# Attention on blocks of four tokens: products of 64 and 68 columns, sums from a column of ones, exponential behind the transposing

## The chip, the cores and the metric

The kernel runs on one core of a Trainium2 chip. The metric is the device time of one execution in microseconds. Before the change the median of nine runs is 490.96 us (483.93 to 496.37).

## The reference

Four conditioned layers act in turn on x, 64 batches of 64 tokens of 256 features, all in fp32; each adds its result to x. The first is a low-rank projection modulated per batch, the second a linear map whose weights are decoded from a condition, the fourth a set of layer norms with gathered gains and an MLP over six concatenated branches. The change is in the third:

```python
kx = modulated_linear(x, s, k_aff_w, k_aff_b, k_w, k_b)
kx = kx.reshape(B, N, H, D)                      # 64 x 64 x 16 x 16
q = k = v = kx
scores = jnp.einsum('bnhd,bnjd->bnhj', q, k) / math.sqrt(D)
A = jax.nn.softmax(scores, axis=-1)
out = jnp.einsum('bnhj,bnjd->bnhd', A, v).reshape(B, N, F)
out = modulated_linear(out, s, o_aff_w, o_aff_b, o_w, o_b)
```

The attention is among the 16 heads of one token: for each of the 4096 tokens a 16x16 matrix of scores from 16 vectors of 16 elements, a softmax over its rows, and its product with the same 16 vectors.

## The kernel before

The 4096 tokens are taken in eight chunks of 512 (`CH`), and behind the keys in 16 units P of 256 (`PT`). `layers01(c)` does the first two layers of a chunk and the keys: it ends with `pt`, the keys of a unit turned so that tokens lie on the partitions, copied to `kk` by ACT. `attention(P)` follows, then `layers23(P)`, which multiplies by the output weights (`po`), norms, gathers, and does the MLP (`ph` for its six branches, `pq` for its second product).

A token's 16x16 products are too small for the tensor engine, so several tokens are put into one product with zeros around them. The keys go to DRAM (`kd`, `vd`) and come back (`fetch`) in the layouts that are needed. Before the change, eight tokens share a product. For the scores, `kb` holds the 128 contraction rows (16 elements x 8 tokens) and, for each of 32 groups, 128 columns (8 tokens x 16 heads), zero but in a token's own block; it is 16 partitions wide per token, so it takes eight transfers (L762). `kz` holds the same keys packed, 32 columns per group with zeros beside, as weights. Two products (h = 0, 1) with weights shifted by 16 columns add up in PSUM; the scores of a unit, `pS`, are 32 products with 32 weight columns and 128 streamed columns, in four column groups of 32 output partitions each (L789). The softmax follows: maximum, difference, exponential on ACT, sum, reciprocal and product on DVE, and a transposing on DVE into `at` (L796 to L803). For the values, `vb` holds 128 columns per group (8 transfers, L767), and `pv` is again 32 products of 128 columns in four column groups (L813); ACT copies it to `av` (L818), `ad` takes it to DRAM (L822), and two transfers bring it back turned as `aT` (L829). Half of what `pv` computes and `ad` carries is not used: only the blocks that belong to a token are read back. `styleq` is the output's modulation in the order of `aT`.

`kb` and `vb` are two halves of one tensor `kv`, which holds the decoder's weights `W_dec` first. There is one of each, so the fetch of unit P+1 must wait until the products of unit P have read them. `at` is one buffer, `kz` two. An fp32 product is two instructions on PE (the trace counts 64 per unit for `pS`).

PSUM has eight banks in four sets: A (2), B (3), C (2) and S (1). `pS` uses S; `pv` and `ph` share the two banks of C.

Nothing is issued as it is written. `Plan.step` takes every step with an engine, a cost, and what it reads and writes; `Plan.order` lays the steps out in time on each engine, choosing among those ready by a rank, which is the unit's base plus `LEAD` of its stage and `SHIFT` of stage and unit, and `emit` writes all the steps in that order. So each engine runs a fixed list in order, and a step that waits holds up those behind it. SP issues all the transfers but the gathers (POOL) and some first loads (ACT).

Of the kernel before, what the change touches and what calls it, by code (L numbers as in the profile page):

```python
# [18 lines left out]
NH, HD = 16, 16  # L19
# [42 lines left out]
class Plan:  # L62
# [3 lines left out]
    LANES, ISSUE, LAND, HOP, SLACK = 8, 0.54, 2.3, 0.12, 0.0  # L66
    TABLE = 1.4

    LEAD = {"down": 946.4, "fetch": 1090.6, "gather": 1168.5, "hidden": 1056.4, "keys": 938.1, "last": 1046.3,
            "load": 934.3, "load W1": 1568.6, "load W2": 1287.4, "load decoder": 1245.0, "load first": 604.2, "load ids": 902.1,  # L70
            "load keys": 911.3, "load states": 1260.1, "load up": 753.0, "mid": 546.9, "norm": 984.7, "out": 1165.7,
            "park": 927.1, "scores": 1120.2, "set W1": 1041.3, "set decoder": 215.9, "set down": 150.6, "set k": 952.6,
            "set o": 868.6, "set states": 1178.6, "turn": 1040.2, "up": 1091.5, "values": -313.8}


    SHIFT = {"down": (121.0, 0.0, -136.0, 0.0, 45.3, 0.0, 57.2, 0.0, 669.8, 0.0, 452.8, 0.0, 448.6, 0.0, 203.0, 0.0),
            "fetch": (-21.2, -95.4, 22.4, 39.5, 73.9, 129.8, -198.4, 143.2, 60.9, 236.7, -128.9, -10.1, -60.7, 22.7, -201.3, -74.5),
            "gather": (25.1, 20.6, -52.3, 44.9, 149.5, 295.4, 273.6, -73.2, 25.2, 4.2, 71.4, 347.0, 156.9, 181.1, 284.4, 233.7),
            "hidden": (-23.7, -102.8, 100.9, 97.4, -70.1, 56.9, 93.3, -244.5, -119.8, 73.4, -11.9, 193.5, 100.1, -16.4, -8.7, 2.5),
            "keys": (-138.5, 0.0, -157.5, 0.0, 320.2, 0.0, 194.1, 0.0, 169.5, 0.0, 259.2, 0.0, 207.7, 0.0, 209.6, 0.0),  # L80
            "last": (-49.6, -146.3, 100.1, 60.6, -162.7, -187.0, 32.8, 25.1, 68.0, -10.7, 96.6, -194.4, -61.8, 407.3, 397.6, 375.4),
            "load": (0.0, 0.0, 0.0, 0.0, 311.2, 0.0, 24.7, 0.0, -364.5, 0.0, 23.9, 0.0, 66.9, 0.0, 299.3, 0.0),
            "mid": (-25.3, 0.0, -351.6, 0.0, -179.2, 0.0, -1.1, 0.0, -6.1, 0.0, 131.7, 0.0, 213.3, 0.0, 249.5, 0.0),
            "norm": (-246.5, -272.7, -139.3, -283.8, -207.2, -15.7, -104.9, 40.1, -219.1, 16.5, -133.9, -101.4, -119.9, 129.5, 13.2, -265.9),
            "out": (75.9, 13.0, -112.7, -113.3, -174.2, 11.1, 82.9, 26.4, 125.1, -118.1, 220.2, -0.8, 136.4, 254.8, -8.3, 195.2),
            "park": (-302.5, 0.0, -53.5, 0.0, -775.7, 0.0, -547.9, 0.0, -550.1, 0.0, -359.8, 0.0, -152.5, 0.0, 238.3, 0.0),
            "scores": (-82.8, 70.4, 67.7, -137.7, -106.8, -38.2, 26.9, 83.3, 98.4, 82.9, 84.9, -0.6, 136.4, 144.2, 34.2, 171.0),
            "turn": (-82.0, 10.3, -20.8, -18.4, -23.5, -0.8, 77.8, 214.9, 84.7, 115.0, -41.3, 77.4, -122.1, 45.8, 69.3, 164.8),
            "up": (-344.7, 0.0, -102.1, 0.0, -238.6, 0.0, -224.7, 0.0, -115.4, 0.0, -84.9, 0.0, -54.9, 0.0, -53.0, 0.0),
            "values": (-74.2, 53.7, -70.1, -159.6, 81.8, 307.5, -59.3, -54.8, 80.6, -145.4, -166.2, -196.3, -101.8, -85.7, -218.8, 125.5)}  # L90
# [12 lines left out]
    @staticmethod  # L103
    def keys(things):
        out = []
        for t in things:
            if isinstance(t, tuple) and isinstance(t[0], Buf):
                out.append((t[0], t[1]))
            else:
                out.append((t, None))  # L110
        return out
# [147 lines left out]
def tile_kernel(ctx: ExitStack, tc: tile.TileContext, a: dict, out: bass.AP):  # L259
# [15 lines left out]
    BUFS = {"x": 3, "xr": 3, "pw": 2, "cg": 2, "mg": 2, "ei": 2, "oh": 2, "t4": 3, "kk": 2, "kc": 1, "act": 2, "E": 2,  # L275
            "aT": 2, "xt": 2, "ft": 2, "hs": 2, "y3": 2, "y1": 1, "mx": 2, "sm": 2, "tab": 2, "st": 2, "mv": 2, "rs": 2, "rsx": 2, "rsh": 2, "rsy": 2, "nmx": 2, "nmh": 2}
# [4 lines left out]
    def bank(name, tag="B"):  # L281
        return Buf(ps, tag, {"A": 2, "B": 3, "C": 2, "S": 1}[tag], [128, 512], name, turns=(tag == "A"))
# [35 lines left out]

    styleq = fixed("styleq", [128, 2, B // PB, 4, 2])
# [14 lines left out]
    kz = [fixed(f"kz{i}", [128, 32 * NG + 16]) for i in range(2)]  # L334

    kv = fixed("kv", [128, 2 * NG * 128])
    kb, vb = (kv[:, i * NG * 128 : (i + 1) * NG * 128].rearrange("p (b g j) -> p b g j", g=NG, b=8) for i in range(2))
    at_ = fixed("at", [128, 32 * NH + 16])


    def consts():
# [4 lines left out]
    step("POOL", 0.4, lambda: (nc.gpsimd.memset(neghalf, -0.5), nc.gpsimd.memset(V, 0.0), nc.gpsimd.memset(bigtab, 0.0),  # L346
                               nc.gpsimd.memset(at_[:, 32 * NH :], 0.0)),
         w=["neghalf", "V", "at0", "zeros"], rank=-107)
    step("POOL", 3.5, lambda: nc.gpsimd.memset(U, 0.0), w=["U"], rank=-108.5)
    for z in range(2):  # L350
        step("POOL", 1.0, lambda z=z: nc.gpsimd.memset(kz[z], 0.0), w=[f"kz{z}"], rank=-106)
# [419 lines left out]
    def parts(n):  # L771
        return [f"{n}.{b}" for b in range(8)]
# [274 lines left out]
```

## Time and profile before

| | |
|---|---|
| median of nine runs | 490.96 us |
| the profiled execution | 487.56 us |
| its span, first to last instruction | 485.8 us |
| mean granted clock of PE | 0.930 |
| DMA packets, bytes | 192668, 83.53 MB |
| of these under 512 B | 159819 |
| SP: `kv<-kd` (L762), 128 issues | 471 / 587 / 2190 ns (least, median, most) |
| SP: `kv<-vd` (L767), 128 issues | 302 / 420 / 1652 ns |
| SP: `vd<-kk` (L744), 64 issues | 582 / 675 / 2894 ns |
| SP: `aT<-ad` (L829), 32 issues | 364 / 505 / 1927 ns |
| ACT: exponential, 128x512 (L798) | 16, 630 ns |
| ACT: copy to `av`, 128x512 (L818) | 32, 590 ns |
| ACT: copy to `kz`, 128x512 (L756) | 16, 618 ns |
| ACT: function table load | 1283 ns each |
| DVE: sum (L799), reciprocal (L800), product (L801) | 684, 351, 690 ns |
| DVE: maximum (L796), difference (L797), transposing (L803) | 686, 691, 707 ns |

Times are those of one profiled execution. PE's row is the matmuls, PEld's the weight loads, which overlap them. A group's mean counts one instruction from start to end, while several are under way at once; its busy time is what they cover together. The waits of an engine are put down to what ended them. The chain of waits runs back from the last instruction, at each step to what released it.

### The profile page before, as it was taken

How to read it: one execution, taken by the hardware profiler on the slowest of the kernel's cores; microseconds unless marked ns; L12 is line 12 of the kernel's file. 1: busy time of each engine (PE TensorE's matmuls, PEld its weight loads, DVE VectorE, ACT ScalarE, POOL GpSimd, SP SyncE). 2: the span in 40 equal slices, each digit the busy share in tenths (PEclk: the TensorE clock that was granted, in tenths of full speed). 3: DMA queues.
4: the chain of work that ended last, by engine and by line, in shares of the span. 5: the costliest groups of instructions: out<-in, count | busy, mean ns of one | idle time of the engine just before them, and what ended most of it. 6: DMA issues, size and time to landing. Idle time of an engine off the chain costs nothing.

```text
span 485.8 us, 11060 instructions
## 1 busy us (share of the span) xinstructions
PE 417.1 (86%) x4026; PEld 317.5 (65%) x4026; DVE 311.9 (64%) x668; ACT 297.2 (61%) x875; POOL 154.2 (32%) x164
## 2 busy tenths in 40 slices
PE   3969859784996899989999998799898988999890
PEld 2956535553773678668777776687666767888770
DVE  0698994541975267587777775759683863886642
ACT  1305815639569465769379738894697964876530
POOL 5470040000436015024613540245132634255110
PEclk9989958976899599989999999999899997999997
DMA  8999676586698768658967897688677777775000
GB/s 271 309 225 276 132 191 153 137 118 152 86 189 234 205 129 201 145 155 230 197 210 115 221 190 191 147 222 131 159 181 252 137 159 208 183 217 156 23 22 22
DMA packets 192668, 83.53 MB, mean 172 GB/s; under 512 B 159819, under 2 KB 174119, under 8 KB 192615
## 3 DMA queue, kind: packets, MB, share of 16 engines
q1 hardware_dynamic: 184679, 57.81, 52.8%
q0 software_dynamic: 6656, 20.98, 15.8%
q10 hardware_dynamic: 1280, 4.05, 2.3%
q8 instruction: 32, 0.52, 0.5%
q14 instruction: 21, 0.17, 0.1%
HBM read 56.91 MB, written 25.89 MB: 170 GB/s over the span
## 4 chain that ended last, share of the span: by engine, by line
PE 51%; DVE 11%; SPq 11%; ACT 11%; DMA 10%; issue 3%; POOLq 0%; POOL 0%; ACTq 0%; DVEq 0%
PE ph L943 18%; PE pv L813 5%; PE pS L789 4%; PE po L883 4%; SPq L767 4%; SPq L762 3%; PE pq L951 3%; DMA kc<-kd 3%; PE pk L707 2%; ACT t L656 2%; PE p L637 2%; DMA aT<-ad 2%; ACT ot L886 2%; DMA kv<-vd 2%; PE pz L688 2%
## 5 line engine op out<-in xcount | busy, mean ns | idle before, releaser
L886 ACT ACTIVATE ot<-po,cols,demod_o 128x64 f32<-128x64 f32 x128 | 41.0, 427 | 14.9 <-PE po L883 14.9
L842 POOL TENSOR_TENSOR rs_x<-rs_x,neghalf 128x2 f32<-128x2 f32 x16 | 13.1, 821 | 115.3 <-DVE rs_x L841 114.8
L856 POOL DMA_INDIRECT mg<-in_ms_tab,ids x32 | 33.8, 1058 | 35.6 <-PE pfs L928 21.0
L710 ACT ACTIVATE kT<-pk,cols,demod_k 128x64 f32<-128x64 f32 x128 | 39.6, 438 | 5.6 <-PE pk L707 3.1
L883 PE MATMUL po<-aS,w_o 128*128 128x256 f32 x128 | 34.7, 419 | 7.9 <-DVE aS L877 7.9
L856 POOL DMA_INDIRECT pw<-in_pw_tab,ids x32 | 34.6, 1082 | 15.4 <-PE pfh L928 7.8
L789 PE MATMUL pS<-kv,kz 128*32 128x128 f32 x1024 | 33.2, 284 | 5.7 <-DMA kv<-vd 3.1
L943 PE MATMUL ph<-fh,W_h 128*128 128x256 f32 x128 | 34.9, 398 | 3.5 <-ACT fh L931 3.4
L943 PE MATMUL ph<-ft,W_t 128*128 128x256 f32 x128 | 35.5, 402 | 1.9 <-ACT ft L931 1.9
L856 POOL DMA_INDIRECT cg<-in_cg_tab,ids x32 | 31.8, 994 | 16.4 <-issue 6.9
L813 PE MATMUL pv<-kv,at 128*32 128x128 f32 x1024 | 33.4, 282 | 2.8 <-DVE at L803 2.5
L789 PEld LDWEIGHTS pS<-kv,kz 128*32 128x32 f32 x1024 | 28.8, 114 | 10.8 <-issue 6.1
L842 POOL TENSOR_TENSOR rs_h<-rs_h,neghalf 128x2 f32<-128x2 f32 x16 | 13.1, 820 | 69.4 <-DVE rs_h L841 69.2
L707 PE MATMUL pk<-xs,w_k 128*128 128x512 f32 x64 | 32.1, 644 | 3.2 <-DVE xs L702 2.3
L883 PEld LDWEIGHTS po<-aS,w_o 128*128 128x128 f32 x128 | 25.9, 208 | 13.7 <-issue 10.0
L951 PE MATMUL pq<-W,hs 128*128 128x256 f32 x128 | 32.4, 390 | 2.0 <-ACT hs L946 1.8
L943 PE MATMUL ph<-fs,W_s 128*128 128x256 f32 x128 | 34.0, 389 | 0.1
L943 PE MATMUL ph<-xr,W_x 128*128 128x256 f32 x128 | 34.0, 389 | 0.0
L813 PEld LDWEIGHTS pv<-kv,at 128*32 128x32 f32 x1024 | 27.9, 113 | 9.1 <-DVE at L803 3.8
L656 ACT ACTIVATE t<-pu,ugT 128x64 f32<-128x64 f32 x128 | 27.6, 381 | 7.8 <-PE pu L651 3.9
L756 ACT COPY kz<-kc 128x512 f32<-128x512 f32 x16 | 9.9, 620 | 34.5 <-DMA kc<-kd 34.5
L943 PEld LDWEIGHTS ph<-fh,W_h 128*128 128x128 f32 x128 | 24.4, 197 | 8.6 <-ACT fh L931 4.9
(228 smaller groups left out, 959.5 us busy)
## 6 DMA issues: line engine op xcount, KB each, us to landing
ad<-av SPq DMA_DIRECT2D x16, 512.0 KB
x<-in_xT SPq DMA_DIRECT2D x8, 512.0 KB
xd<-x SPq DMA_DIRECT2D x8, 512.0 KB
xr<-xd SPq DMA_DIRECT2D x16, 256.0 KB
kd<-kk SPq DMA_DIRECT2D x32, 128.0 KB
vd<-kk SPq DMA_DIRECT2D x64, 64.0 KB
kc<-kd SPq DMA_DIRECT2D x16, 256.0 KB
kv<-kd SPq DMA_DIRECT2D x128, 32.0 KB
```

The costliest lines, as they stand in the source:

```text
L656: nc.scalar.activation(t1()[:, d, h * 256 + b * S : h * 256 + (b + 1) * S], pu[h]()[:, d * 256 + b * S : d * 256 + (b + 1) * S], AF.Copy, ...
L707: step("PE", 1.82, lambda o=o: [mm(pk[o](), wT["k"][:, k, o * 128 : (o + 1) * 128], xs()[:, k, :], start=(k == 0), stop=(k == 1)) for k in ...
L710: nc.scalar.activation(kT()[:, o, b * S : (b + 1) * S], pk[o]()[:, b * S : (b + 1) * S], AF.Identity, scale=demod["k"][:, o, b0 + b : b0 + ...
L767: step("SP", 0.50, lambda b=b: nc.sync.dma_start(vb[b * 16 : (b + 1) * 16, b].rearrange("p g d -> p (g d)"), vd()[b].rearrange("h g d -> h ...
L789: mm(pS()[32 * cc : 32 * cc + 32, r * 128 : (r + 1) * 128], kzt[:, g * 32 + 16 : g * 32 + 48] if h == 0 else kzt[:, g * 32 : g * 32 + 32], ...
L813: mm(pv[h]()[32 * q : 32 * q + 32, r * 128 : (r + 1) * 128], at_[:, c0 : c0 + 32], vb[:, :, q * 8 + h * 4 + r, :], start=True, stop=True)
L842: step("POOL", 1.25, lambda: nc.gpsimd.tensor_tensor(rs(), rs(), neghalf[:, 0:2], ALU.pow), r=["neghalf"], w=[rs], rank=rank)
L856: step("POOL", 1.35, lambda dst=dst, tab=tab, i=i, t=t: nc.gpsimd.indirect_dma_start(out=dst()[:, t, :], out_offset=None, in_=a[tab], in_o ...
L883: step("PE", 1.74, lambda: [mm(po()[:, o * PT : (o + 1) * PT], wT["o"][:, k, o * 128 : (o + 1) * 128], aS()[:, k, :], start=(k == 0), stop ...
L886: step("ACT", 1.16, lambda o=o: [nc.scalar.activation(ot()[:, o, b * S : (b + 1) * S].rearrange("p (z s) -> p z s", z=2), po()[:, o * PT : ...
L943: mm(dst(), W1[n][:, k, o * 128 : (o + 1) * 128], rhs()[:, k, :], start=False, stop=(n == "h" and k == 1))
L951: step("PE", 0.90, lambda t=t: [mm(pq()[:, t * D : (t + 1) * D], hs()[:, k, t * 128 : (t + 1) * 128], W2[:, k, :], start=(k == 0), stop=(k ...
```

## The change

- The scores of four tokens share a product. The 128 contraction rows are 16 elements x 2 halves (`t`) x 4 tokens; the weights `kz` hold the keys of two tokens side by side with a mask (`tmask`, a new input of 128x2, loaded once), so that no second product has to be added: 32 products with 64 streamed columns instead of 32 with 128.
- `kb` and `vb` become two of each (`kb[z]`, `vb[z]`, z = P % 2). `kb` is fetched in 4 transfers of 32 rows instead of 8 of 16.
- `vd` and `vb` carry a one behind each 16 elements (17 columns per head, from `vk`, two buffers that are set to one at the start). The product `pv` of 68 columns then has the softmax's sum in each block's 17th column. The reciprocal of it and the product with it are done on DVE out of `pv`, in the place of ACT's copies to `av`.
- The exponential comes behind the transposing: DVE transposes the differences to `Et`, and two activations on ACT, each on 64 partitions, write the exponentials into the blocks of `at` (whose other blocks are zero from the start).
- `av` and `ad` are half as long; `aT` is read in eight pieces of 32 tokens per row instead of four of 64. Tokens come out in their own order, so `styleq` goes.
- The planner's `keys` takes tuples of names as well, `SLACK` is 0.1 instead of 0, bank S is given out in turns, and `LEAD` and `SHIFT` have other numbers.

```diff
-    LANES, ISSUE, LAND, HOP, SLACK = 8, 0.54, 2.3, 0.12, 0.0
+    LANES, ISSUE, LAND, HOP, SLACK = 8, 0.54, 2.3, 0.12, 0.1
...
-            if isinstance(t, tuple) and isinstance(t[0], Buf):
+            if isinstance(t, tuple):
...
-    kz = [fixed(f"kz{i}", [128, 32 * NG + 16]) for i in range(2)]
-    kv = fixed("kv", [128, 2 * NG * 128])
-    kb, vb = (kv[:, i * NG * 128 : (i + 1) * NG * 128].rearrange("p (b g j) -> p b g j", g=NG, b=8) for i in range(2))
-    at_ = fixed("at", [128, 32 * NH + 16])
+    kz = [fixed(f"kz{i}", [128, NG, 2, NH]) for i in range(2)]
+    WK, WV = 4 * NG * HD, 4 * NG * (HD + 1)
+    kv = fixed("kv", [128, 2 * WK + 2 * WV])
+    kb = [kv[:, z * WK : (z + 1) * WK].rearrange("p (b g j) -> p b g j", g=NG, b=4) for z in range(2)]
+    vb = [kv[:, 2 * WK + z * WV : 2 * WK + (z + 1) * WV].rearrange("p (b g j) -> p b g j", g=NG, b=4) for z in range(2)]
+    vk = [fixed(f"vk{i}", [128, 2, NH, HD + 1]) for i in range(2)]
+    tmask = fixed("tmask", [128, 2])
+    at_ = fixed("at", [128, NG, 2, NH])
...
+            for e in range(2):
+                for cc in range(2):
+                    def f(e=e, cc=cc, p=p, vd=vd):
+                        src = vk[p][2 * e + cc : 2 * e + cc + 1]
+                        src = bass.AP(src.tensor, src.offset, [[4 * src.ap[0][0], 32], [HD + 1, 2 * NH], [1, HD + 1]])
+                        nc.sync.dma_start(vd()[cc, e].rearrange("h g d -> g h d"), src)
...
+        for t in range(2):
+            step("ACT", act(512), lambda t=t: nc.scalar.activation(kz[z][:, :, t, :], kc(), AF.Copy, scale=tmask[:, t : t + 1]), r=[kc, "tmask"],
+                 w=[f"kz{z}.{t}"], rank=rank)
+        for b in range(4):
+            def f(b=b):
+                dst = kb[z][b : b + 1, b % 2 * 2 + b // 2]
+                nc.sync.dma_start(bass.AP(dst.tensor, dst.offset, [[4 * pitch, 32], [1, NG * NH]]),
+                                  kd().rearrange("d t (x g) h -> x (d t) (g h)", x=4)[b])
...
         def f():
-            for r in range(4):
-                for h in range(2):
-                    for cc in range(4):
-                        g = h * 16 + r * 4 + cc
-                        mm(pS()[32 * cc : 32 * cc + 32, r * 128 : (r + 1) * 128],
-                           kzt[:, g * 32 + 16 : g * 32 + 48] if h == 0 else kzt[:, g * 32 : g * 32 + 32],
-                           kb[:, :, g, :], start=(h == 0), stop=(h == 1))
+            for g8 in range(8):
+                for cc in range(4):
+                    g = g8 * 4 + cc % 2 * 2 + cc // 2
+                    mm(pS()[32 * cc : 32 * cc + 32, g8 * 64 : (g8 + 1) * 64], kz[z][:, g].rearrange("p a h -> p (a h)"), kb[z][:, :, g, :],
+                       start=True, stop=True)
...
-        step("ACT", act(512), lambda: nc.scalar.activation(E(), E(), AF.Exp, scale=1.0 / 4.0), w=[E], rank=rank, table="exp")
-        step("DVE", vec(512), lambda: nc.vector.tensor_reduce(sm(), E(), AX.X, ALU.add), r=[E], w=[sm], rank=rank)
-        step("DVE", 0.39, lambda: nc.vector.reciprocal(sm(), sm()), w=[sm], rank=rank)
-        step("DVE", vec(512), lambda: nc.vector.tensor_tensor(E(), E(), rep(sm(), NH), ALU.mult), r=[sm], w=[E], rank=rank)
-        step("DVE", vec(512), lambda: nc.vector.transpose(at_[:, 0 : 32 * NH], E().rearrange("p g j -> p (g j)")), r=[E], w=["at"], rank=rank)
+        Et = sb("E", [128, NG, NH], f"Et_{P}")
+        step("DVE", vec(512), lambda: nc.vector.transpose(Et().rearrange("p g i -> p (g i)"), E().rearrange("p g j -> p (g j)")), r=[E], w=[Et], rank=rank)
+        for h in range(2):
+            step("ACT", act(512), lambda h=h: nc.scalar.activation(
+                at_[64 * h : 64 * h + 64, :, h, :], Et()[64 * h : 64 * h + 64], AF.Exp, scale=1.0 / 4.0), r=[Et, "at"], w=[f"at.{h}"], rank=rank, table="exp")
...
-        av = sb("av", [128, HD, 2, 2, 4, 4], f"av_{P}")
-        for z in range(2):
-            step("ACT", act(512), lambda z=z: nc.scalar.copy(
-                av()[:, :, :, z],
-                pv[z]().rearrange("p (r c l d) -> p d l r c", r=4, c=4, d=HD)), r=[pv[z]], w=[(av, z)], rank=rank)
+        av = sb("av", [128, HD, 2, 16], f"av_{P}")
+                        mm(pv[h]()[32 * q : 32 * q + 32, s4 * 68 : (s4 + 1) * 68], at_[:, g8 * 4 + q].rearrange("p c h -> p (c h)"),
+                           vb[z][:, :, q % 2 * 16 + q // 2 * 8 + g8, :], start=True, stop=True)
+            pvv = lambda h=h: pv[h]()[:, 0:272].rearrange("p (g d) -> p g d", d=HD + 1)
+            step("DVE", 0.25, lambda h=h, pvv=pvv: nc.vector.reciprocal(sm()[:, h * 16 : (h + 1) * 16], pvv()[:, :, HD]), r=[pv[h]], w=[(sm, h)], rank=rank)
+            step("DVE", vec1(256), lambda h=h, pvv=pvv: nc.vector.tensor_tensor(
+                view(av(), [[1, 8], [16, 2], [32, HD]], h * 8), pvv()[:, :, 0:HD].rearrange("p (s y) d -> p s y d", y=2),
+                rep(sm()[:, h * 16 : (h + 1) * 16].rearrange("p (s y) -> p s y", y=2), HD), ALU.mult), r=[pv[h], (sm, h)], w=[(av, h)], rank=rank)
+        ad = Buf(dram, "ad", 4, [128, HD, 32], f"ad_{P}")
```

## The prediction

> **What bounds the kernel now.** I read the page's busy table first, for which engine could be the bound at all:
>
> ```profile
> PE 417.1 (86%) x4026; PEld 317.5 (65%) x4026; DVE 311.9 (64%) x668; ACT 297.2 (61%) x875; POOL 154.2 (32%) x164
> ```
>
> Only PE is near full. An average over stages says little, so next the busy times by stretch of about 61 us (columns: length, then PE, PEld, DVE, ACT, POOL busy with instruction counts, granted clock, DMA share, GB/s):
>
> ```profile
> 55.00:121.00 66.00, 47.56 (x469) 29.85 (x466) 35.52 (x70) 34.89 (x117) 5.82 (x7) 0.79 0.70 144
> 121.00:182.00 61.00, 54.61 (x546) 40.57 (x548) 38.37 (x83) 39.23 (x117) 19.00 (x19) 0.89 0.76 168
> 182.00:243.00 61.00, 58.72 (x622) 44.90 (x619) 44.87 (x93) 40.67 (x115) 24.15 (x25) 0.97 0.78 186
> 243.00:304.00 61.00, 58.68 (x584) 44.05 (x582) 43.30 (x91) 44.28 (x137) 19.63 (x20) 1.00 0.79 185
> 304.00:365.00 61.00, 54.71 (x623) 42.58 (x623) 43.40 (x94) 46.47 (x135) 21.93 (x24) 0.97 0.74 170
> 365.00:425.00 60.00, 53.20 (x591) 43.95 (x590) 37.15 (x88) 43.92 (x115) 23.36 (x26) 0.94 0.76 187
> ```
>
> From 182 to 304 PE is busy 96% of the time: there a microsecond less of PE is a microsecond less of span. From 55 to 182 PE has 25 us of gaps. What fills them is seen in the chain that ended last:
>
> ```profile
> PE 51%; DVE 11%; SPq 11%; ACT 11%; DMA 10%; issue 3%; POOLq 0%; POOL 0%; ACTq 0%; DVEq 0%
> PE ph L943 18%; PE pv L813 5%; PE pS L789 4%; PE po L883 4%; SPq L767 4%; SPq L762 3%; PE pq L951 3%; DMA kc<-kd 3%; PE pk L707 2%; ACT t L656 2%; PE p L637 2%; DMA aT<-ad 2%; ACT ot L886 2%; DMA kv<-vd 2%; PE pz L688 2%
> ```
>
> The two products the change rewrites (pS, pv) hold 9.4% of the chain, 45.7 us, and the issues of their operands (SP's queue at L762 and L767) another 6.8%, 33 us. The costs of the products come from the groups by shape; the third row is the nearest relative of what they become:
>
> ```profile
> L813 PE MATMUL pv<-kv,at 128*32 128x128 f32 x1024 | 33.4, 282 | 2.8 <-DVE at L803 2.5
> L789 PE MATMUL pS<-kv,kz 128*32 128x128 f32 x1024 | 33.2, 284 | 5.7 <-DMA kv<-vd 3.1
> L678 PE MATMUL py<-x,U 128*32 128x64 f32 x256 | 9.0, 224 | 3.9 <-DVE ys_noi L571 2.4 <-DVE x L668 1.5
> ```
>
> Each fp32 product is two instructions, so 64 per half batch of 256 tokens ("unit") for pS and for pv.
>
> **PE, the main term.** In the trace's records at full clock the four column groups (outputs 32q) start 6 to 7 ns apart and the next four 109 ns later: 16 sets of 109 = 1.745 us per unit. py has the same 32-column weights, but 64 columns streamed and two groups: a pair every 56 ns. So a set lasts as long as its stream. After the change pS streams 64 columns in four groups, 16 x 56 = 0.90; pv streams 68, 16 x 59.5 = 0.95. Saved per unit: 0.85 + 0.80 = 1.65; over 16 units 26.4 us.
>
> That needs eight instructions (four loads, four matmuls) in 56 ns, 7 ns each, kept up for 0.9 us. Could weight loads forbid it? pU's 128-column loads follow each other every 112 ns, 28 ns for 32 columns; one after another, four would take 112 ns a set and nothing would be won. Against that, the start of one pS burst (length, PE and PEld busy with instructions seen in the stretch, clock):
>
> ```profile
> 260.05:260.11 0.06, 0.05 (x4) 0.05 (x8) 1.00 0.13 6
> ```
>
> Eight loads and four matmuls begin within 60 ns, 5 ns each; in sequence the loads alone would take 224. So groups load side by side, and issue reaches the rate in a burst. Whether it lasts over 128 instructions no row shows: the fastest sustained rate is 64 pairs in 1.745 us. Bounds of the gain: 0 and 26.4; I take 26.4, because py, the nearest row, follows its stream.
>
> The Trainium skill speaks against this: "TensorE: Matmul & The Clock Gate", section "Wait — 56ns, not 53.3ns?", says starts never come closer than about 25 ns however few columns are streamed. The 6 to 7 ns between groups already differ from it here. By the page 64 x 25 = 1.60 us per product and unit would be left, an estimated gain of 4.6 us instead of 26.4.
>
> How much lies on the path: in 182-365 and 425-474 PE is busy 219 of 232 us; 8 pS and 9 pv lie there, 8 x 0.85 + 9 x 0.80 = 14.0, counted whole. The other 12.4 lie where PE is busy 83%; I count half, 6.2 (bounds 0 and 12.4). **-20.2.**
>
> **SP's queue.** kb comes in 4 issues instead of 8: 64 fewer at a median of 587 ns, 38 us of queue. On the chain L762 has 3.3%, 16 us; half goes, 8, and with PE next behind I count half of that, 4 (bounds 0 and 8). vb keeps 128 issues of 420 ns, now with two pieces per row; between nothing and the 505 ns of aT's issue (four pieces per row) that is 0 to 11 us of queue, a quarter of it on the chain as today (17 of 65): 0 to 3, taken 1. Net **-3**. kb and vb get a second buffer: today SP waits 4.6 us for pS and pv to give them up (2.0 + 2.0 + 0.6 among its waits); half: **-2**.
>
> **Order.** The ranks are new, and the listed orders show what moves. The first fetch of tab stands 44 issues behind the last store of tabd, after the change 11. On the chain that fetch is a 6.84 us landing at 154.9. PE has 6.4 us of gaps in that stretch: 0 to 6, taken **-2**. ACT switches its function table 29 times instead of 26: 3 x 1.283 = 3.8 us.
>
> **ACT and DVE.** ACT loses 32 copies of av (590 ns, 18.9 us), gains 16 masked copies of kc (618) and 16 more exponentials (630; half the partitions, the same length): 20.0. With the table loads ACT grows by 4.9 us; it is busy 61%, under PE. Bounds 0 and 4.9; taken **+1**. DVE loses per unit the sum (684), a reciprocal (351) and the product (690), 1.725; it gains two reciprocals of 16 columns (0.25 each, on the line through 351 at 32 and 944 at 128 columns) and two 256-wide products (0.42, as L645): 1.34. That is 6 us less of DVE. From pS to pv the chain of steps drops from 4.45 to 3.34 us per unit. Both count nothing: they are covered by the ph products of other units; if that cover is gone, up to 1.1 us a unit is won. The memsets of the attention's buffers at the start change from 9.0 to an estimated 9.1 us on POOL (862 ns per 1024 columns), beside the loads; nothing.
>
> **DMA.** By the packet records 64 B takes 10.3 ns, 256 B 18. vd's 65,536 pieces grow to 68 B: 0 to 31 us over 16 engines. aT's 16,384 pieces of 256 B become 32,768 of 128 B, at 14 each +10; ad's halve, 171 to 113 ns, -7. The share (0.70 to 0.79) rises by at most 0.08. On the path stands only aT's landing, 1.8%, 8.7 us: -1 to +4, taken **+1**.
>
> **Sum**: -20.2 - 3 - 2 - 2 + 1 + 1 = -25.2. The profiled execution took 487.56 (span 485.8 and 1.8 around it): 462.4. The median of the runs, 490.96, is 1.007 of it: 465.6, so **465 us**.
>
> **Rivals.**
> - *Issue-bound products.* If the sequencer can't sustain more than today's 27 ns per pair, the main term goes to 0, and with it nearly everything: what is left is -5, 486; at twice today's rate all of it comes. For it: no sustained row below 27 ns. Against it: the 5 ns burst. Part of the way, 478 to 486.
> - *DVE holds the banks (slower).* pv is now emptied by DVE instead of ACT. Its two PSUM banks are those of ph, and both engines run in order: a reciprocal behind other work on DVE holds the next ph or pv on PE, and behind the wait for pv stand DVE's xr and pw steps, which feed PE. Today ACT waited for pv in 15 of 32 copies, so banks were freed at once. Price: each 512-wide step queued ahead is 0.69 us, times 32 emptyings 22 us. It decides from 25.2 / 32 = 0.79 us per emptying; with two steps ahead 44 - 25 = +19, 510. Against it: DVE is busy at most 74% of any stretch above, and in the listed order the reciprocal follows on a single step such as oh (336 ns), act (424), y (686) or xs (1.22 us), not on a queue of them.
> - *Clock.* A stall of a few us is followed by PE at half clock: a mean of 0.93 is some 68 us at half. Fewer PE instructions mean longer gaps; 20 us more at half clock cost 10. This is width of the range, not a case.
>
> **Numbers.** Forecast 0.76, with its own range 448 to 478; issue-bound 0.13; DVE's hold 0.11. 80%: 448 (the halves counted whole) to 485 (the issue-bound case). 1% of the median is the least that a measurement tells from no change: faster means below 486. All but little of the forecast, two thirds of the issue-bound case: 0.84; same 0.08, slower 0.08 (most of the hold).
>
> **What would show it.** Right: the rows of pS and pv near 1.1 us a unit (0.9 and the last matmul's length), 17 to 19 each instead of 33; PE near 391; starts of a set 56 ns apart; SP's issues of kb 64. Wrong: rows of 28 and more (issue), idle of PE before ph or pv ended by the new reciprocal or product on DVE (hold), a granted clock well below 0.93, or aT's landings longer on the chain. If PE's busy time falls by 26 and the span by less than 15, my count of halves was wrong and the gaps grew instead.

## The result and the profile after

The changed kernel takes 565.84 us (median, 559.19 to 577.85), beside 485.65 us of the kernel before on the same chips: a ratio of 1.1672 (95% interval [1.1634, 1.1711]). Here and below a ratio compares the quicker executions of both kernels, since some executions of any kernel run a few per cent longer, while a median counts them all. The kernel is 17% slower where 5% faster was forecast. The profiled execution took 581.58 us, the longest of all; it has a span of 579.8 us, 94.0 more than before, and a mean granted clock of 0.868 instead of 0.930.

First the page of the changed kernel, its busy times and its chain of waits (shares of the span by engine, then by line):

```profile
PE 440.8 (76%) x4026; PEld 326.8 (56%) x4026; DVE 306.2 (53%) x680; ACT 307.8 (53%) x878; POOL 156.5 (27%) x166
...
PE 37%; DMA 25%; ACT 17%; SPq 12%; issue 4%; DVE 3%; another core or an unknown queue 0%; POOLq 0%; ACTq 0%; POOL 0%; DVEq 0%
PE ph L946 13%; DMA vd<-vk 10%; DMA kc<-kd 10%; PE pU L473 4%; SPq L748 4%; PE pq L954 4%; SPq L740 3%; ACT junk L838 3%; ACT kT L712 3%; PE pv L818 2%; ACT t L657 2%; PE pk L709 2%; ACT kz L763 2%; PE p L638 2%; SPq L773 2%
```

DMA has gone from 10% of the chain to 25%. `vd`'s writing, which was not among the chain's lines before, holds 10%, and the landing of `kc` has gone from 3% to 10%. PE's idle time (span less busy) has doubled, from 68.7 to 139.0 us, and PE's busy time has grown by 23.7 although the products are shorter. The clock's records are all 1.0 or 0.5: 155.3 us of them lie at half clock, 70.2 before. PE was busy in 97.9 us of that time, before in 46.9; half of the 51.0 more, some 25 us, is an estimate of what the lower clock added to PE's busy time. So the 94.0 us are 70.3 of idle and 23.7 of busy time. In the latter the rows of `pS` and `pv` fell by 20.9 and PE's other products grew by some 44, which the clock explains in part.

The costliest groups by line show which wait it is (busy us, mean ns of one, idle of the engine before them and what ended it):

```profile
L763 ACT ACTIVATE kz<-kc,tmask 128x512 f32<-128x512 f32 x32 | 21.6, 721 | 88.3 <-DMA kc<-kd 88.3
...
L818 PE MATMUL pv<-kv,at 128*32 128x68 f32 x1024 | 23.3, 245 | 29.5 <-ACT at L807 11.1
...
L795 PE MATMUL pS<-kv,kz 128*32 128x64 f32 x1024 | 22.4, 250 | 27.6 <-ACT kz L763 27.4
```

Before the change the first of these waits was shorter:

```profile
L756 ACT COPY kz<-kc 128x512 f32<-128x512 f32 x16 | 9.9, 620 | 34.5 <-DMA kc<-kd 34.5
```

ACT waited 34.5 us for `kc`; now it is 88.3, and PE waits behind ACT. The products themselves are down from 33.2 and 33.4 us to 22.4 and 23.3 in spite of the lower clock. The chain's pieces in order of time (start, length, what) have nothing like these before, where no write of `vd` is among the longest:

```profile
99.49 9.77 DMA vd<-vk
110.59 7.25 DMA vd<-vk
...
142.79 11.00 DMA vd<-vk
...
166.49 13.56 DMA vd<-vk
```

The waits for these writes of 68 KB take 7 to 14 us. In the same order of work with pieces of 64 bytes (the second experiment below), the two that stand on the chain take 3.0 and 3.7 us, so it is no matter of 4 bytes more. The records of the single packets, counted by size (mean ns, 50th, 95th and 99th percentile, and their sum over the 16 engines in us), say where:

```
                     mean   p50  p95   p99   sum/16
before, 64 B         10.3    11   14    19     84.2   (131,200: kd and vd)
after,  64 B (kd)    12.0    11   11    44     49.1
after,  68 B (vd)    28.2    12   89   435    115.7   (65,536)
before, 2048 B      113.4    84  267   555     72.6
after,  2048 B      127.4    84  368   828     81.6
```

The median packet of 68 B costs 12 ns, one more than 64 B. The tail makes the mean: one in a hundred takes over 435 ns. By windows of 72 us (PE, PEld, DVE, ACT, POOL busy, then clock, DMA share, GB/s):

```profile
144.00:216.00 72.00, 54.71 (x484) 39.98 (x486) 34.46 (x81) 40.00 (x126) 18.29 (x19) 0.83 0.94 132
216.00:288.00 72.00, 53.51 (x568) 38.67 (x564) 41.33 (x89) 44.03 (x117) 18.94 (x19) 0.86 1.00 142
288.00:360.00 72.00, 50.35 (x527) 36.61 (x520) 40.12 (x86) 37.75 (x105) 24.38 (x25) 0.87 0.89 138
```

Before the change the same windows had:

```profile
144.00:216.00 72.00, 63.36 (x698) 46.66 (x696) 42.31 (x89) 48.98 (x143) 18.76 (x20) 0.91 0.72 178
216.00:288.00 72.00, 70.87 (x700) 54.45 (x692) 54.34 (x114) 52.60 (x162) 33.67 (x33) 1.00 0.82 191
288.00:360.00 72.00, 65.01 (x720) 49.66 (x716) 49.08 (x105) 51.99 (x152) 19.84 (x22) 0.98 0.75 177
```

The DMA share has risen to 0.89 to 1.00 and the bytes moved have fallen to 132 to 142 GB/s. The DMA engines are occupied, not productive.

### The profile page after: what moved, and what is told of

Read it like the earlier page. It is cut to its first block, busy times and chain, and to the rows that moved or that the text cites. A ratio compares the mean times of both kernels' runs of the same rounds, so it can differ in the third digit from the quotient of the medians.

```text
span 579.8 us, 11005 instructions
## 1 busy us (share of the span) xinstructions
PE 440.8 (76%) x4026; PEld 326.8 (56%) x4026; DVE 306.2 (53%) x680; ACT 307.8 (53%) x878; POOL 156.5 (27%) x166
## 4 chain that ended last, share of the span: by engine, by line
PE 37%; DMA 25%; ACT 17%; SPq 12%; issue 4%; DVE 3%; another core or an unknown queue 0%; POOLq 0%; ACTq 0%; POOL 0%; DVEq 0%
PE ph L946 13%; DMA vd<-vk 10%; DMA kc<-kd 10%; PE pU L473 4%; SPq L748 4%; PE pq L954 4%; SPq L740 3%; ACT junk L838 3%; ACT kT L712 3%; PE pv L818 2%; ACT t L657 2%; PE pk L709 2%; ACT kz L763 2%; PE p L638 2%; SPq L773 2%
## 5 line engine op out<-in xcount | busy, mean ns | idle before, releaser
L763 ACT ACTIVATE kz<-kc,tmask 128x512 f32<-128x512 f32 x32 | 21.6, 721 | 88.3 <-DMA kc<-kd 88.3
L818 PE MATMUL pv<-kv,at 128*32 128x68 f32 x1024 | 23.3, 245 | 29.5 <-ACT at L807 11.1
L795 PE MATMUL pS<-kv,kz 128*32 128x64 f32 x1024 | 22.4, 250 | 27.6 <-ACT kz L763 27.4
L860 POOL DMA_INDIRECT mg<-in_ms_tab,ids x32 | 34.5, 1079 | 25.8 <-PE pfs L931 14.8
L946 PE MATMUL ph<-ft,W_t 128*128 128x256 f32 x128 | 38.4, 428 | 3.4 <-ACT ft L934 3.3
L818 PEld LDWEIGHTS pv<-kv,at 128*32 128x32 f32 x1024 | 18.9, 122 | 38.8 <-ACT at L807 12.9
L709 PE MATMUL pk<-xs,w_k 128*128 128x512 f32 x64 | 36.6, 716 | 3.4 <-DVE xs L703 2.9
L822 DVE RECIPROCAL sm<-pv 128x16 f32<-128x16 f32 x32 | 8.1, 254 | 58.0 <-PE pv L818 56.5
L860 POOL DMA_INDIRECT cg<-in_cg_tab,ids x32 | 33.5, 1046 | 19.2 <-issue 6.6
L946 PE MATMUL ph<-fs,W_s 128*128 128x256 f32 x128 | 37.2, 417 | 1.3 <-ACT fs L934 1.3
L795 PEld LDWEIGHTS pS<-kv,kz 128*32 128x32 f32 x1024 | 19.2, 130 | 33.5 <-ACT kz L763 29.5
L946 PE MATMUL ph<-xr,W_x 128*128 128x256 f32 x128 | 37.0, 416 | 0.0
```

The lines of the kernel that those rows point to most:

```text
L709: step("PE", 1.82, lambda o=o: [mm(pk[o](), wT["k"][:, k, o * 128 : (o + 1) * 128], xs()[:, k, :], start=(k == 0), stop=(k == 1)) for k in ...
L763: step("ACT", act(512), lambda t=t: nc.scalar.activation(kz[z][:, :, t, :], kc(), AF.Copy, scale=tmask[:, t : t + 1]), r=[kc, "tmask"], w= ...
L795: mm(pS()[32 * cc : 32 * cc + 32, g8 * 64 : (g8 + 1) * 64], kz[z][:, g].rearrange("p a h -> p (a h)"), kb[z][:, :, g, :], start=True, stop ...
L818: mm(pv[h]()[32 * q : 32 * q + 32, s4 * 68 : (s4 + 1) * 68], at_[:, g8 * 4 + q].rearrange("p c h -> p (c h)"), vb[z][:, :, q % 2 * 16 + q ...
L860: step("POOL", 1.35, lambda dst=dst, tab=tab, i=i, t=t: nc.gpsimd.indirect_dma_start(out=dst()[:, t, :], out_offset=None, in_=a[tab], in_o ...
L946: mm(dst(), W1[n][:, k, o * 128 : (o + 1) * 128], rhs()[:, k, :], start=False, stop=(n == "h" and k == 1))
```

## The experiments

The theory at this point: the odd pieces of `vd` stall the queues, and all else follows. The rivals: the new order of the work, the changed products or softmax steps. The first four kernels stand beside a median of the kernel before of 490.54 us.

**One part alone.** The kernel before, with 68-byte pieces in `vd` (`VD` is `HD + 1`, in `vb` too), the ones left unused; products, softmax and order stay.

```diff
-            vd = vds[P] = Buf(dram, "vd", 2 * NC, [8, NH, NG, HD], f"vd_{P}")
+            vd = vds[P] = Buf(dram, "vd", 2 * NC, [8, NH, NG, VD], f"vd_{P}")
...
-                           vb[:, :, q * 8 + h * 4 + r, :], start=True, stop=True)
+                           vb[:, :, q * 8 + h * 4 + r, 0:HD], start=True, stop=True)
```

> The kernel before with one part of the change alone: vd's pieces and vb's columns are 17 elements (68 bytes) instead of 16; the products still read 16. Theory A (the 68-byte pieces stall the DMA queues, as the after-trace's 28.2 ns a packet against 10.3 before suggests): 540 to 580 us, packets of 68 bytes at 20 ns or more in the mean, kc's landings on the chain. Theory B (the new order of the planner's ranks, or the other parts of the change, made it slow): 480 to 492 us, packets near 11 ns.

585.89 us, ratio 1.2144 [1.2021, 1.2268], a little above the first theory's range: this part alone makes the kernel before slower than the whole change does. In the trace PE, DVE, ACT and SP do their work in the same order as before. Its groups show the same wait:

```profile
L760 ACT COPY kz<-kc 128x512 f32<-128x512 f32 x16 | 9.9, 620 | 107.2 <-DMA kc<-kd 107.2
```

The 68-byte packets have a mean of 25.4 ns (p99 383), and the clock is 0.863.

**That part undone.** The changed kernel with 64-byte pieces and no ones; `pv` has 64 columns and the reciprocal is taken of a value, so the softmax's division is left out.

```diff
-    WK, WV = 4 * NG * HD, 4 * NG * (HD + 1)
+    VD = HD
+    WK, WV = 4 * NG * HD, 4 * NG * VD
...
```

> The changed kernel with 64-byte pieces again: no ones behind the values, pv has 64 columns, and the reciprocal is taken of the 16th value in place of the sum (the softmax's division by its sum is left out). Theory A: 450 to 480 us, packets of 64 bytes near 11 ns. Theory B: 550 to 570 us, as with 68 bytes.

486.36 us, by the medians 0.991 of before: the slowdown is gone, with the order, the products and the softmax of the change in place. But so is the forecast gain.

**Size or place.** The same kernel with its 64-byte pieces written 4 bytes further on (the division is left out here too).

```diff
-    VD = HD
+    VD, OFF = HD, 1
...
+                        nc.sync.dma_start(bass.AP(t.tensor, t.offset + OFF + (cc * 2 + e) * VQ, [[VD, 32], [32 * VD, 2 * NH], [1, VD]]), src)
```

> As the kernel with 64-byte pieces, but vd begins 4 bytes later in DRAM, so that each piece lies across a 64-byte boundary and shares a line with its neighbour (the same parts of the computation are left out). If it is the position (lines shared by two pieces) that stalls: 540 to 580 us, packets of 64 bytes at 20 ns or more. If it is the size of 68 bytes: as with 64-byte pieces, 450 to 480 us. Theory B: 550 to 570 for both.

587.2 us, ratio 1.2054 [1.1858, 1.2249]. Not a byte more is moved, and it is as slow as with 68 bytes: 64-byte packets 22.8 ns in the mean (p99 329) instead of 10.8, though this counts `kd`'s pieces too, which stay where they were. It is the place, not the size. In this run `vd` is also read back from 4 bytes further on. The reads are not needed for the stall: the changed kernel reads rows of 1088 bytes from multiples of 32, and a buffer below that nobody reads shows a stall as well.

**A first repair.** The complete kernel with 64-byte pieces; the ones lie in a fifth block that `vb[0]` and `vb[1]` share, so `pv` streams 80 columns. It also has one buffer instead of two for `st` and `mv`, and one DVE step more, so the planner laid out another order.

```diff
+    vw = [kv[:, 2 * WK + z * WV : 2 * WK + z * WV + WV + WO].rearrange("p (b g j) -> p b g j", g=NG, b=5) for z in range(2)]
...
-                        mm(pv[h]()[32 * q : 32 * q + 32, s4 * 68 : (s4 + 1) * 68], at_[:, g8 * 4 + q].rearrange("p c h -> p (c h)"),
+                        mm(pv[h]()[32 * q : 32 * q + 32, s4 * 80 : (s4 + 1) * 80], at_[:, g8 * 4 + q].rearrange("p c h -> p (c h)"),
```

> The changed kernel, complete, with the ones in a fifth block of vb that is written once (shared by the two buffers), 64-byte pieces in vd, and 80 columns in pv instead of 68. Theory A: 455 to 485 us (pv's sets 69 ns instead of 59: 2.5 us more in all than with 64-byte pieces and 64 columns), faster than the kernel before. Theory B: 555 to 575 us.

523.16 us, ratio 1.0811 [1.0614, 1.1008], between the two ranges, though the packets are back at 10.3 ns. A second cause was at work here; a later run narrows it down.

Now the second question: why is there so little gain without the odd pieces? (before: 494.75)

**The main term by itself.** The kernel before, in its own order, with `pS` and `pv` streaming 64 of their 128 columns; half of each product is left out, the two products of `pS` no longer add up, and ACT's copy repeats the columns that are there.

```diff
-                           kb[:, :, g, :], start=(h == 0), stop=(h == 1))
+                           kb[:, h * 4 : h * 4 + 4, g, :], start=True, stop=True)
...
-                           vb[:, :, q * 8 + h * 4 + r, :], start=True, stop=True)
+                           vb[:, 0:4, q * 8 + h * 4 + r, :], start=True, stop=True)
```

> The kernel before, order and all else the same, with only the streams of its products halved: pS and pv stream 64 columns instead of 128 (half of each product is left out). Theory P (26 us less of PE lie mostly on the path, as I counted): 461 to 476 us. Theory Q (PE's time in the products isn't what the span waits for; SP, ACT, DVE and the landings stand right behind it): 479 to 490 us. PE's rows of pS and pv near 20 us each instead of 33 in both.

488.84 us, ratio 0.997 [0.9907, 1.0032]. Its busy times, its groups on PE and two of its windows:

```profile
PE 406.5 (83%) x4026; PEld 302.7 (62%) x4026; DVE 307.8 (63%) x668; ACT 296.1 (61%) x875; POOL 155.5 (32%) x164
...
L813 PE MATMUL pv<-kv,at 128*32 128x64 f32 x1024 | 21.8, 230 | 6.2 <-DVE at L803 3.2 <-issue 2.0 <-ACT hs L946 0.9
L789 PE MATMUL pS<-kv,kz 128*32 128x64 f32 x1024 | 21.4, 238 | 5.1 <-DMA kv<-kd 4.0 <-issue 1.1
```

```profile
182.00:243.00 61.00, 56.76 (x677) 42.76 (x665) 47.80 (x99) 42.44 (x121) 25.64 (x26) 0.97 0.77 187
243.00:304.00 61.00, 53.77 (x581) 39.77 (x580) 42.05 (x87) 42.34 (x131) 19.62 (x20) 1.00 0.84 198
```

The rows of `pS` and `pv` fell from 66.6 to 43.2 us, 23.4 less, and the span did not move (487.3 beside 485.8). PE's busy time fell by only 10.6, since its other products grew by 12.7: 98.7 us lie at half clock instead of 70.2, and PE was busy in 69.7 of them instead of 46.9 (half of that difference is 11.4). And idle grew by 12.1. So about half of the saving went to the clock and about half to waiting. In 243 to 304, where PE was 96% busy before and the clock is 1.00 in both, 58.68 us of PE (584 matmuls) became 53.77 (581), and the rest became waiting. A PE at 96% was not alone on the path there: the next wait stood right behind it.

**The order.** The changed kernel with 64-byte pieces (the division left out) and the `LEAD`, `SHIFT` and `SLACK` of before.

```diff
-    LANES, ISSUE, LAND, HOP, SLACK = 8, 0.54, 2.3, 0.12, 0.1
+    LANES, ISSUE, LAND, HOP, SLACK = 8, 0.54, 2.3, 0.12, 0.0
...
-            "park": 659.3, "scores": 1200.4, "set W1": 1513.1, "set decoder": 246.5, "set down": 7.3, "set k": 821.4,
+            "park": 927.1, "scores": 1120.2, "set W1": 1041.3, "set decoder": 215.9, "set down": 150.6, "set k": 952.6,
```

> The changed kernel with 64-byte pieces (the division by the softmax's sum left out) and the planner's ranks and slack of before. Theory R (the new order gave the gain of the products back): 455 to 475 us. If the order is not at fault: 478 to 500 us.

508.66 us, above both ranges and by the medians 1.028 of before, against 0.991 with the new numbers: the new order serves the changed kernel; it is not the cause.

**The repair in the change's own order.** The complete kernel with the fifth block again, all buffers kept, and the ones put there within a POOL step that exists already.

```diff
-    WK, WV = 4 * NG * HD, 4 * NG * (HD + 1)
-    kv = fixed("kv", [128, 2 * WK + 2 * WV])
+    WK, WV, WO = 4 * NG * HD, 4 * NG * HD, NG * HD
+    VO = 2 * WK + WV
+    kv = fixed("kv", [128, 2 * WK + 2 * WV + WO])
...
+        if n == "vb1":
+            nc.gpsimd.tensor_copy(kv[:, VO : VO + WO].rearrange("p (g j) -> p g j", j=HD)[:, :, 0:4],
+                                  bass.AP(tmask.tensor, tmask.offset + 2, [list(tmask.ap[0]), [0, NG], [1, 4]]))
```

> The changed kernel, complete, ones in a shared fifth block of vb, 64-byte pieces; this time every step has the planner's cost and order of the changed kernel, and only what the steps do differs. If the first such kernel's 523 us came from its other order: 482 to 495 us, as with 64-byte pieces. If from the 80 columns or from the fifth block: 515 to 530 us.

483.76 us, ratio 0.9861 [0.9729, 0.9994]: faster than both kernels, and 39 us less than the first repair with the same products and the same pieces. DMA holds 6% of its chain. The eighty columns and the fifth block cost nothing that shows beside the kernel without them (0.991 above, 0.980 below by the medians); the first repair's loss lay in its order or its two single buffers, which no run separates.

**Who the neighbour is.** The kernel 4 bytes past (the division left out), its pieces laid so that neighbours in DRAM come from one partition.

```diff
-[[VD, 32], [32 * VD, 2 * NH], [1, VD]]
+[[2 * NH * VD, 32], [VD, 2 * NH], [1, VD]]
```

> 64-byte pieces that begin 4 bytes past a line, as in the run with the moved vd, but laid so that pieces that share a line come from one partition, and so from one DMA engine, but at the partitions' ends (values are in another order, so the attention's result is another). If pieces of different engines in one line stall each other: 480 to 500 us and packets of 64 bytes near 11 ns. If a piece across a line is slow by itself or next to its own neighbour: 570 to 600 us and 20 ns or more.

728.75 us, ratio 1.4897 [1.4624, 1.5169]; packets 35.9 ns. Neither number that was expected. It takes no writers of two partitions to hold each other; neighbours of one are worse. In SBUF its pieces stand 68 bytes apart, so that they stay packets of 64 bytes; the last experiment has the same on the grid.

**How coarse the grid is** (before: 492.65). 32 and 64 bytes past instead of 4, the division left out.

```diff
-    VD, OFF = HD, 1
+    VD, OFF = HD, 8
```

and 16 in the second.

> The 64-byte pieces of vd (the softmax's division left out, as in the run at 4 bytes past) begin 32 bytes late, so each still shares a 64-byte line with its neighbour, but no word of 32 bytes is shared. If lines of 64 bytes are what stalls, 64-byte packets have a mean of 20 ns or more and the time is 560 to 600 us; if only words of 32 bytes matter, packets have 10 to 12 ns and the time is 480 to 500 us.

> The control: the pieces begin 64 bytes late and share nothing of 64 bytes, but a row of pieces no longer begins at a multiple of 128 bytes or more. Lines of 64 bytes: packets of 10 to 12 ns, 480 to 500 us. Lines of 128 bytes or more, or the start of the buffer: 560 us or more.

477.63 us (ratio 0.9777 [0.9666, 0.9889]) and 471.36 us (0.965 [0.9543, 0.9758]); packets 12.2 and 10.6 ns (p99 48 and 29). 32 bytes past, every piece still shares its 64 bytes with a neighbour, and hardly anything stalls. So multiples of 32 bytes are grid enough; 8 and 16 bytes were not tried, so "word" below means 32 bytes at most.

**Product time put back** (the same before). The complete repaired kernel with each set of four matmuls of `pS` and `pv` issued twice:

```diff
-            for g8 in range(8):
+            for g8 in [i // 2 for i in range(16)]:
...
-                for s4 in range(4):
+                for s4 in [i // 2 for i in range(8)]:
```

> The complete changed kernel with the ones in a shared fifth block and 64-byte pieces (483.8 us, 0.986 of before), with every set of four matmuls of pS and pv issued twice: nothing is left out, 27 us of product time are put back (64 pairs more per product and unit; rows of pS and pv from about 20 us each to 33 or 34). If a microsecond of products less was a microsecond of time less, as the prediction counted, the time rises by 20 us or more, to 504 or above, ratio 1.03 or more. If the products' time is paid for by the clock and the gaps either way, the time rises by less than 10 us, ratio 0.98 to 1.00, and the time at half clock falls by as much as PE's busy time grows, while the granted clock stays or rises.

493.65 us, ratio 1.0081 [1.0019, 1.0143], 0.022 ± 0.015 above the ratio of the same kernel without it, on another chip: 11 ± 7 us of 490, between the two expectations. From the page of an execution of 510.35 us:

```profile
PE 449.4 (88%) x6074; PEld 347.0 (68%) x6074; DVE 306.5 (60%) x680; ACT 307.5 (60%) x878; POOL 156.4 (31%) x166
...
L826 PE MATMUL pv<-kv,at 128*32 128x80 f32 x2048 | 44.5, 246 | 8.4 <-ACT at L815 3.9
...
L803 PE MATMUL pS<-kv,kz 128*32 128x64 f32 x2048 | 34.9, 226 | 4.8 <-ACT kz L771 2.7
```

The rows grew from 25.6 and 19.2 to 79.4 together, 34.6 us. So a microsecond of these products is worth about a third of a microsecond of time, a rough number by the interval. That execution has 62.9 us at half clock, beside 66.9 without the second issue. But the executions behind the ratio were granted more: 0.941 to 0.959, beside 0.926 to 0.932. By 2 x (1 - clock) x span that is an estimated 45 us at half clock beside 68, and beside 59 in the best version below. So the time at half clock fell by 14 to 23 us, a third to a half of what PE's busy time grew (45 us).

**The best version, and the spread** (before: 484.17). The complete repair with `vd` 64 bytes further on; the 64-byte kernel with only the longer buffer; and that kernel once more (the division left out in both).

```diff
-            vd = vds[P] = Buf(dram, "vd", 2 * NC, [2, 2, 2 * NH, 32, HD], f"vd_{P}")
+            vd = vds[P] = Buf(dram, "vd", 2 * NC, [1, 4 * 2 * NH * 32 * HD + 16], f"vd_{P}")
...
+                        nc.sync.dma_start(bass.AP(t.tensor, t.offset + 16 + (cc * 2 + e) * VQ, [[HD, 32], [32 * HD, 2 * NH], [1, HD]]), src)
```

> The complete changed kernel with the ones in a shared fifth block and 64-byte pieces (ratio 0.986), its vd beginning 64 bytes later in a buffer 64 bytes longer. If the placement is what made the like run 471 us, ratio 0.96 to 0.97, 470 to 478 us. If that was the spread between runs, ratio 0.98 to 0.99, 481 to 488 us.

> As the run 64 bytes past (the softmax's division left out), with the longer buffer but the pieces at its start. If the offset counts, 481 to 490 us, as the 64-byte pieces without it; if the length (where the buffers behind it lie) counts, 467 to 476 us.

> The changed kernel with 64-byte pieces and without the softmax's division once more, beside the others on one chip: 481 to 490 us, ratio 0.98 to 1.00, if it differs from the run 64 bytes past by its placement; 468 to 478 us, ratio 0.96 to 0.97, if the earlier difference was one of chips and runs.

470.83 us (ratio 0.9791 [0.9698, 0.9884]), 470.8 (0.9704 [0.9592, 0.9817]) and 474.48. The last was 486.36 beside a before of 490.54; the same kernel has 0.991 and 0.980 of its before by the medians. So offset and length do nothing that shows, and the earlier difference was spread. The first is complete and beats both kernels. Its busy times, groups and windows show what the change looks like without the odd pieces (the ones stand in the fifth block):

```profile
PE 391.5 (84%) x4026; PEld 290.5 (62%) x4026; DVE 304.8 (65%) x680; ACT 307.0 (66%) x878; POOL 154.5 (33%) x166
...
L773 ACT ACTIVATE kz<-kc,tmask 128x512 f32<-128x512 f32 x32 | 21.7, 730 | 29.2 <-DMA kc<-kd 29.2
...
L835 DVE TENSOR_TENSOR av<-pv,sm 128x256 f32<-128x256 f32 x32 | 18.9, 599 | 5.8 <-DMA ad<-av 4.7 <-DVE sm L832 0.2
...
L805 PE MATMUL pS<-kv,kz 128*32 128x64 f32 x1024 | 17.8, 221 | 4.9 <-ACT kz L773 4.4 <-DMA kv<-kd 0.6
```

```profile
144.00:216.00 72.00, 66.08 (x773) 50.45 (x772) 49.72 (x115) 54.71 (x147) 27.88 (x29) 1.00 0.81 194
216.00:288.00 72.00, 66.23 (x797) 48.53 (x799) 56.35 (x117) 57.60 (x157) 25.19 (x26) 1.00 0.82 181
288.00:360.00 72.00, 62.93 (x660) 46.56 (x650) 46.70 (x109) 55.18 (x169) 26.02 (x28) 0.93 0.83 168
```

Against the same windows of the changed kernel: 11 to 13 us more of PE in each, the clock back at 0.93 to 1.00, DMA at 0.81 to 0.83 with 168 to 194 GB/s instead of 132 to 142.

**A cut word or a shared one** (before: 481.63). The 64-byte kernel (division left out) writes each piece of `vd` a second time into a buffer `vz` at a pitch of 128 bytes that nobody reads, on the grid and 4 bytes past (the line below); and the kernel with neighbours from one partition is put on the grid.

```diff
+                        nc.sync.dma_start(bass.AP(t.tensor, t.offset + 1 + (cc * 2 + e) * 64 * NH * 32, [[32, 32], [32 * 32, 2 * NH], [1, HD]]), src)
```

> The kernel with 64-byte pieces (the softmax's division left out) writes each piece of vd a second time, to a buffer that nobody reads, at a pitch of 128 bytes, on the grid: 65,536 packets more of 64 bytes, 64 issues more on SP. The price of the extra work: 42 us over 16 engines and 64 x 0.7 us of SP's queue, 490 to 540 us, 64-byte packets still at 10 to 12 ns.

> As the last, the extra pieces 4 bytes past the grid: each begins and ends within a 32-byte word, and no word is shared, since 64 bytes lie between them. If the cut words alone stall, 64-byte packets have a mean of 15 ns or more and the time is 60 us or more above the run on the grid; if it takes two packets in one word, the mean stays at 10 to 12 ns and the time within 15 us of it.

> The run whose neighbours in DRAM came from one partition, now on the grid. If sharing a word made its 728.75 us, the time is 465 to 500 us and packets have 10 to 12 ns; if its order of writing is slow by itself, 600 us or more.

555.76, 604.36 and 470.99 us (the first ratio 1.154 [1.1455, 1.1624], the last 0.9763 [0.9677, 0.9849]). The last is clean: 10.3 ns, so its order of writing and its 68-byte steps in SBUF cost nothing on the grid, and the 258 us it lost 4 bytes past come of words that were cut and shared. The second's three executions, 592.04 to 604.66 us, lie 36 to 49 us above the first's, in the same order of work: cut words stall without a neighbour too, but less. By the packets, the 65,536 cut and unshared ones added 27.4 us over 16 engines (156.1 against 128.7); cut and shared ones added 98 (186.6 against 88.2), and those of one partition 210 (294.0 against 84.5 on the grid). Both answers hold in part. That the extra writes on the grid cost about 80 us is far more than was expected; `vz`'s steps also made the planner lay out another order, and the two weren't separated.

## Why the prediction was wrong

**The step that failed: "DMA. ... vd's 65,536 pieces grow to 68 B: 0 to 31 us over 16 engines ... On the path stands only aT's landing ... taken +1."** It priced a packet by its size, between the rows of 64 and 256 B. All pieces of 64 B before the change start at multiples of 64 in their buffers, so the rows could not show what a piece off the 32-byte grid costs. 68-byte packets had 28.2 ns instead of the 10.3 to 18 allowed; their sum grew by 73 us (115.7 less 42.2 for 65,536 at 10.3), not by 31; the DMA share rose by 0.14 to 0.22 in the windows shown, not 0.08. And it was on the path: `vd`'s writing became 10% of the chain, and the transfers behind it were held up, `kc`'s above all. The term was +1; the experiments put it at 80 to 100 us: 565.84 after beside 470.83 and 483.76 repaired (88 to 91 us by the ratios), and +95 alone in the kernel before.

The Trainium skill has a rule near this one: "Collectives: The Full Stack", section "Rules for kernel authors", wants the buffers of collectives aligned to 32 bytes, to prevent a read-modify-write by the hardware. The packets of this case fit such a grid (12.2 ns at 32 bytes past, 22.8 at 4); that the stall is a read-modify-write no run shows. "DMA: Bandwidth & Descriptors", section "Specifications", puts the read-modify-write at everything under 512 B. Here packets of 64 B on the grid ran at 10.3 ns with a 99th percentile of 28 in the very layout that had 35.9 and 576 at 4 bytes past, so the size alone did not make the tail.

**PE, the main term.** The mechanism was right, and the rate with it: at full clock the four groups of a set start 6 to 7 ns apart and the next set 35 to 36 (pS) or 39 (pv) later, 56 and 59.5 ns per set, kept up over a unit. Repaired, `pS` has 17.8 and 19.2 us where 17 to 19 was said. That PE's busy time is 391.5 where 391 was said is in part luck: that execution was granted a clock of 0.951, and the other repaired one has 404.4 at 0.932. The issue-bound rival is out. What was mis-sized is the -20.2 "on the path": counted whole in 182-365 and 425-474 because PE was busy there, and half elsewhere. The two runs on it give 1.5 ± 3 us for 23.4 us of product time in the old order, and 11 ± 7 for 34.6 in the new one. The repaired kernel gained 7 and 10 us of 491 in all (ratios 0.9861 and 0.9791). The forecast's own last sentence named the sign, PE down by 26 and the span by less than 15; the profiled executions have -25.6 and -18.8, the timed runs -10.

**SP's queue, double buffers, order: -3, -2, -2.** Together they can't be told from nothing. With the products issued twice, the complete kernel has 12.8 us more product time than before (79.4 less 66.6), a third of which is 4 us, and it is 4 us slower: the rest sums to about zero within some 4 us, an estimate that takes the third as given. The order's -2 went the other way in one place: PE waits 6.8 us for a fetch of `tab` in the best version, beside 1.5 before; the repair in the change's own order shows no such wait. ACT's 29 table loads came as counted.

**ACT +1, DVE 0.** The masked copy takes 710 to 722 ns in the median, not the 618 of the plain one; ACT's busy time grew by 9.8 us in the repaired kernel instead of 4.9. DVE's product out of `pv` takes 599 ns, not 420, in the best version; DVE's total fell by 7.1, near the 6 worked out. Neither engine bounds.

**The rivals.** "DVE holds the banks" did not happen: its PE waits on the new reciprocal and product come to 1.3 us in the changed kernel and at most 2.1 in its repaired forms. The slower side was right for no reason that the prediction gave. "Clock" was named as width of the range only; in the changed kernel it is some 25 us by the estimate above. The granted clock of 0.868 is one of the signs of being wrong that the forecast listed; that the longer waits brought it about is argued, not shown.

What stays open: how the products' lost gain divides between the clock and the next wait. The old order showed both (28.5 us more at half clock, 12.1 more idle), and with products put back the estimated time at half clock fell by 14 to 23 us; but no run held the clock. Open too are what happens inside the chip at a cut word, whether 8 or 16 bytes would do as a grid, and what made the first repair slow.

## What to carry to other kernels

Before a row of small DRAM pieces is widened, look where each piece starts and ends: pieces that cut a 32-byte word cost far more than their bytes, and three to four times as much in packet time where two pieces share it; put the extra value elsewhere on the chip instead. A saving on an engine that is 96% busy is not its path share: look which wait stands next behind it, and halve one product alone before believing the sum. A rare, long packet is seen in the packets' 99th percentile and in a DMA share that rises while GB/s fall, not in a median.

## What the hardware showed unexpectedly

- One value per head moved the kernel by some 80 us, and other transfers slowed with it: 2048-byte packets, whose own layout is the same, have 127.4 ns, 102.6 in the best repaired kernel and 172.5 with neighbours from one partition.
- Where the packets of one issue of 68-byte pieces run without another's (stretches parted by gaps of 0.3 us or more), five of six have 10 to 11 ns each and one 23; where four issues run together, 24 to 43. Mostly the stall needs company.
- Four column groups start 6 to 7 ns apart and keep up 14 ns per 64-column matmul with its load over a whole unit.
- The same kernel had medians of 486.36 and 474.48 us on two occasions, with 490.54 and 484.17 for the kernel before, 0.991 and 0.980: even such a ratio does not settle a per cent.
